# Residual sums and step-size sums as identity passes on TensorE, in a two-layer Metaformer kernel

## The chip, the cores and the metric

The kernel runs on one core of one Trainium2 chip. The metric is device time in microseconds; it is the time of one launch. The core has five engines that each work through their own queue in order: TensorE (PE), VectorE (DVE), ScalarE (ACT), GpSimd (POOL) and SyncE (SP), which issues the transfers.

## The reference

The input is an image batch `x` of shape (4, 64, 64, 128), float32. Two layers follow, each of a mixing part and a feed-forward part, all with residuals:

```python
x = x + L0_conv(ln_c(x))      # state-space scans over the image in 4 directions
t = tokens(x)
t = t + L0_ffn(ln_t(t))       # 64 experts with a global gate: top 8 tokens pooled and scattered
x = image(t)
x = x + L1_conv(ln_c(x))      # self, row-sum and column-sum projections
t = tokens(x)
t = t + L1_ffn(ln_t(t))       # 16 spectral filters of length 4096, and 3 shifted projections
```

In the scans each of 4 directions has 256 channels with 16 states and 4096 positions. The step size of a channel at a position is a softplus, and the state follows a recurrence:

```python
delta = softplus(dts + dt_bias)
h = exp(delta * A) * h + (delta * u) * B     # for each of 16 states
y = sum over states of h * C
```

## The kernel before, in words

**Stages.** Each image passes through `before_scans` (norm, projection, 3x3 convolution, projections to B, C and the step sizes' inputs), `gate`, the scans, `after_scans` (sum of directions, norm, gate, projection to 128 channels, residual), `experts_and_sums` (gate, pooled tokens, experts, scatter with a residual, then layer 1's mixing with a residual and the shifted projections), `to_slots`, the filters (`convolve`) and `from_slots`. Only `before_scans(0)` runs alone at the head. Then come the scans of all four images, and beside image b's scans runs a list of other stages, `beside(b)` (L1262): beside image 0 the first stages of images 1 to 3, `gate` for images 0 to 2 and `filters()`, which only prepares constants; beside image b > 0 the stages `after_scans`, `experts_and_sums` and `to_slots` of image b - 1, and then eight groups of `convolve`. "The filters" below means `convolve`. After the scans, in the tail, image 3's later stages run among the other 40 groups of `convolve`.

**The scans.** They are cut into 128 chunks (4 images x 4 directions x 8 pieces of 512 positions), each with 16 steps, one for each state; the loop over the 2048 steps starts at L1395. In a step s: SP loads `bc` for s + 5; ACT makes `da` for s + 3 (L1412, two halves, five buffers); DVE multiplies `db` = `du` x B (L1440) and runs two recurrences into `hh` (L1446, six buffers); POOL saves the last state of step s - 1 (L1455) and multiplies its `hh` by C (L1456); PE adds step s - 2 into `y` in PSUM by transposing passes (L1482). At the end of a chunk ACT copies `dx` of the next chunk into `du` in PSUM (`into_psum`, L1389); `du` and `db` have one buffer each.

**The step sizes.** `step_sizes` (L1292) makes the next chunk's `dl` (step sizes) and `dx` (`dl` times the channel's input `xc`) in small pieces, one at the start of each step from step 1 on: transfers at step 1; two projections on PE (L1311) with two reads by ACT each (L1315, L1316) at steps 2 and 3; three ACT operations of width 1024 at steps 4 to 6; at step 7 a POOL subtraction `ex` (L1337) and ACT's Ln into `w` (L1338); at step 8 POOL's `w` + `ex` (L1340); at step 9 POOL's `dl` + `w` (L1342); at step 10 POOL's product `dx` (L1344). The next chunk's first `da` is issued at step 13.

**Dealing.** The stages are generators that yield a weight after each piece of work. `deal` (L1361) is called twice a step, in the middle and at the end of the step's passes into `y`; it hands out pieces until an image's share is due, and orders them behind the step's own instructions on each engine. The share is `WEIGHT[b]` (L35), the sum of a list's weights, spread over the deals. The first chunk of an image and steps 2 and 3 of every chunk (`FIRST`, `BUSY`) get none; there `deal` returns at its top, before anything else.

**PSUM beside the scans.** `slots(ones, twos)` (L209) gives the dealt stages two single banks (`ones`), or one double bank (`twos`) in `convolve`, which switches at its beginning and its end. `bank` (L232) hands out a bank. An eviction from PSUM is put in a list by `evict_soon` (L226) and queued later by `settle` (L222), at the next deal or the next bank.

**Residuals.** Three residuals are POOL additions of an evicted projection: in `after_scans` `project` (L563) evicts to `pr` and L590 adds it to `xr`, which is then stored to `x1_d`; in `experts_and_sums` `scatter` (L929) evicts to `sc` and L950 adds it to `x2`; `mix` (L979) evicts to `zs` and L1041 adds it to `x2`. `pipelined` (L278) runs each such list of steps as a software pipeline over the row groups, the later steps first.

Of the kernel before, what the change touches and what calls it, by code (L numbers as in the profile page):

```python
# [17 lines left out]
P = 128  # L18
# [10 lines left out]
SC = 512  # L29
# [2 lines left out]


FIRST = 1
WEIGHT = (1346.0, 2087.0, 2005.0, 2059.0)  # L35

BUSY = (2, 3)

# [40 lines left out]
def kernel(  # L79
# [126 lines left out]

    side = {"tail": False, "deals": False}

    def slots(ones, twos):  # L209
        if "pool" in side:  # L210
            side["pool"].close()
        side["pool"] = ExitStack()
        for name, n in (("ones", ones), ("twos", twos)):
            side[name] = n and side["pool"].enter_context(
                tc.tile_pool(name=f"side_{name}", bufs=n, space=PSUM)
            )

    soon = []  # L220
# [5 lines left out]
    def evict_soon(work):  # L226
        if side["deals"]:
            soon.append(work)
        else:
            work()  # L230

    def bank(shape, name):  # L232

# [273 lines left out]
    def after_scans(b):  # L507

        with tc.tile_pool(name="po", bufs=2) as po:
            yk, y, z, xr, st, yT, pr = {}, {}, {}, {}, {}, {}, {}  # L510

            def rows(g):
                return slice(256 * g, 256 * (g + 1))

            def load(g):
                for k in range(K):
                    t = po.tile([P, 2, DI], F32, name=f"yk{k}")
                    yk[g, k] = t
                    if k % 2 == 0:
                        src = y_d[b][k, rows(g), :].rearrange("(q p) d -> p q d", p=P)  # L520
                        nc.sync.dma_start(t, src)
                    else:
                        byc = y_d[b][k].rearrange("(w q i) d -> i w q d", w=W, i=2)
                        for i in range(2):
                            nc.sync.dma_start(
                                t[i * W : (i + 1) * W], byc[i][:, 2 * g : 2 * g + 2]
                            )

            def add(g):
                ps = bank([P, 2, DI], "yk_ps")  # L530
                for k in range(K):
                    nc.tensor.matmul(ps, ident, yk.pop((g, k)), start=(k == 0), stop=(k == K - 1))  # L532
                y[g] = po.tile([P, 2, DI], F32, name="y", bufs=8)
                evict_soon(lambda: evict(y[g], ps))

            def sums(g):
                st[g] = norm_sums(po, y[g], 2, DI, eps5)

            def apply(g):
                z[g] = po.tile([P, 2, 256], F32, name="z", bufs=5)  # L540
                nc.sync.dma_start(z[g], z_d[b][:, :, rows(g)].rearrange("h p l -> p h l"))
                xr[g] = po.tile([P, 2, C], F32, name="xr", bufs=9)
                nc.sync.dma_start(xr[g], x[b, rows(g), :].rearrange("(q p) c -> p q c", p=P))
                norm_apply(y[g], y[g], st[g], 2)

            def turn(g):
                yT[g] = po.tile([P, 2, 256], F32, name="yT", bufs=4)
                ps = bank([P, 2, 2, P], "yt_ps")
                for h in range(2):
                    for q in range(2):  # L550
                        nc.tensor.transpose(
                            ps[:, h, q, :], y[g][:, q, h * P : (h + 1) * P], ident
                        )
                for h in range(2):
                    nc.scalar.activation(
                        yT[g][:, h, :],
                        ps[:, h].rearrange("p q t -> p (q t)"),
                        AF.Identity,
                        bias=nb[:, h : h + 1],
                        scale=nw[:, h : h + 1],  # L560
                    )

            def project(g):  # L563
                ps = bank([P, 2, C], "pr_ps")
                for q in range(2):
                    for h in range(2):
                        nc.tensor.matmul(
                            ps[:, q, :],
                            yT[g][:, h, q * P : (q + 1) * P],
                            w_out_t[:, h, :],  # L570
                            start=(h == 0),
                            stop=(h == 1),
                        )
                pr[g] = po.tile([P, 2, C], F32, name="pr")
                evict_soon(lambda: evict(pr[g], ps))

            yield from pipelined(
                16,
                (1.0, load),
                (2.2, add),  # L580
                (2.0, sums),
                (1.2, lambda g: norm_refine(po, st[g], 2, DI, 1e-5)),
                None,
                (1.2, apply),
                None,
                (1.0, turn),
                (1.2, lambda g: nc.gpsimd.tensor_mul(yT[g], yT[g], z[g])),
                None,
                (1.2, project),
                (0.7, lambda g: nc.gpsimd.tensor_add(xr[g], xr[g], pr[g])),  # L590
                (
                    0.4,
                    lambda g: nc.sync.dma_start(
                        x1_d[b][rows(g), :].rearrange("(q p) c -> p q c", p=P), xr[g]
                    ),
                ),
            )
# [114 lines left out]
    def experts_and_sums(b):  # L712

        with tc.tile_pool(name="mk", bufs=1) as kp:
# [203 lines left out]
            with tc.tile_pool(name="l1", bufs=2) as lp:  # L918
# [2 lines left out]
                mm = lp.tile([P, H], F32, name="mm", bufs=1)  # L921
                mk = lp.tile([P, 2, W], F32, name="mk", bufs=1)
                with tc.tile_pool(name="l1a", bufs=2) as la:
                    sc, st, xn = {}, {}, {}

                    def x4(g):
                        return x2[:, 4 * g : 4 * g + 4, :]

                    def scatter(g):  # L929
                        ps = bank([P, 4, C], "sc_ps")  # L930
                        for q in range(4):
                            t0 = 512 * g + q * P
                            nc.tensor.matmul(
                                ps[:, q, :], pT[:, t0 : t0 + P], outE, start=True, stop=True
                            )
                        sc[g] = la.tile([P, 4, C], F32, name="sc")
                        evict_soon(lambda: evict(sc[g], ps))

                    def sums(g):
                        st[g] = norm_sums(la, x4(g), 4, C, eps6)  # L940
# [1 line left out]
                    def apply(g):  # L942
# [3 lines left out]
                    yield from pipelined(  # L946
                        8,
                        (0.4, lambda g: nc.sync.dma_start(x4(g), tiles(x1_d[b], g))),
                        (1.5, scatter),
                        (1.2, lambda g: nc.gpsimd.tensor_add(x4(g), x4(g), sc[g])),  # L950
                        (3.0, sums),
                        (1.2, lambda g: norm_refine(la, st[g], 4, C, 1e-6)),
                        None,
# [17 lines left out]
                yield LAG  # L971

                with tc.tile_pool(name="l1b", bufs=2) as lb:
                    zs, st2, u, uT, ar = {}, {}, {}, {}, {}

                    def x2g(g):
                        return x2[:, 2 * g : 2 * g + 2, :]

                    def mix(g):  # L979
                        ps = bank([P, 2, C], "z_ps")  # L980
                        for q in range(2):
                            r0 = 4 * g + 2 * q
                            pq = ps[:, q, :]
                            t0 = r0 * W
                            nc.tensor.matmul(pq, xT[:, t0 : t0 + P], wself_t, start=True, stop=False)  # L985
                            nc.tensor.matmul(
                                pq, mk.rearrange("p i w -> p (i w)"), wk_t, start=False, stop=False
                            )
                            for i in range(2):
                                nc.tensor.matmul(  # L990
                                    pq[i * W : (i + 1) * W],
                                    mm[:, r0 + i : r0 + i + 1].to_broadcast([P, W]),
                                    wm_t,
                                    start=False,
                                    stop=True,
                                )
                        zs[g] = lb.tile([P, 2, C], F32, name="zs")
                        evict_soon(lambda: evict(zs[g], ps))

                    def sums2(g):  # L1000
                        st2[g] = norm_sums(lb, x2g(g), 2, C, eps5)
# [15 lines left out]
                    def regress(g):  # L1017
# [19 lines left out]

                    yield from pipelined(
                        16,
                        (1.8, mix),  # L1040
                        (0.7, lambda g: nc.gpsimd.tensor_add(x2g(g), x2g(g), zs[g])),  # L1041
                        (1.6, sums2),
                        (1.2, lambda g: norm_refine(lb, st2[g], 2, C, 1e-5)),
                        None,
# [235 lines left out]
    with ExitStack() as c0:  # L1280
# [11 lines left out]
        def step_sizes(b, k, ci):  # L1292
# [6 lines left out]
            def pieces():  # L1299
# [37 lines left out]
                nc.gpsimd.tensor_sub(ex, ex, dx)  # L1337
                nc.scalar.activation(w, w, AF.Ln)  # L1338
                yield
                nc.gpsimd.tensor_add(w, w, ex)  # L1340
                yield
                nc.gpsimd.tensor_add(dl, dl, w)  # L1342
                yield
                nc.gpsimd.tensor_mul(dx, dl, xc)  # L1344

            return dl, dx, xc, pieces()
# [14 lines left out]
        def deal(*behind):  # L1361


            if i % (K * NSC) < FIRST or s >= total or s % N in BUSY:
                return
            start = len(traced)
            settle()
            share["due"] += WEIGHT[chunks[i][0]] / ((K * NSC - FIRST) * (N - len(BUSY)) * 2)
            while share["made"] < share["due"]:
                share["made"] += next(share["pieces"], 1e9)  # L1370
# [256 lines left out]
```

## Time and profile before

| | |
|---|---|
| Runs | 11200.63, 11200.73, 11202.45 us; median 11200.73 |
| Profiled execution | 11189.8 us |
| Its span, first to last instruction | 11188.0 us |
| Mean granted TensorE clock | 0.83 |
| Busy: PE | 8372.3 us (75%) |
| Busy: DVE | 8145.9 us (73%) |
| Busy: ACT | 6173.9 us (55%) |
| Busy: POOL | 7262.3 us (65%) |
| Scan steps, first to last | about 290 to 9006 us |
| `convolve` beside the scans | about 3600 to 4640, 5700 to 6800, 7860 to 9006 us |

An engine's busy time is the time in which it works on an instruction. In the views, a line such as `hh L1446` names the tile that is written and the line of the kernel; `A <- B` means that A waited until B was done; in a list of waits the numbers are the total in us, how many there were, and the longest. In a timeline each row has the start, the duration, the engine, the line, what is written from what, the shape and how many instructions were merged; square brackets hold the idle time just before it and what ended it. A row of 40 digits is the busy share, in tenths, in 40 equal slices of the span.

### The profile page before, as it was taken

What the parts mean: (1) busy time and instruction counts of PE and PEld (TensorE: products, weight loads), DVE (VectorE), ACT (ScalarE), POOL (GpSimd) and SP (SyncE); (2) the same over time, 40 slices, a digit from 0 to 9 for tenths busy, and PEclk for the clock granted to TensorE, in tenths of its full rate; (3) what the DMA queues carried; (4) which work ended last, traced back from release to release, by engine and by line L of the source; (5) the groups of instructions that cost most, each with busy time, mean ns of one, the idle gap of its engine ahead of it and who ended that gap; (6) DMA issues with size and microseconds to landing.
All of it is one profiled execution on the core that took longest, in us unless ns stands there. A gap on an engine that the chain in (4) does not pass through costs nothing. (4 is left out here: it accounts for less than half of the span.)

```text
span 11188.0 us, 117102 instructions
## 1 busy us (share of the span) xinstructions
PE 8372.3 (75%) x34656; PEld 4820.6 (43%) x34656; DVE 8145.9 (73%) x7046; ACT 6173.9 (55%) x12043; POOL 7262.3 (65%) x6518
## 2 busy tenths in 40 slices
PE   6677676546766777657677776576677789999999
PEld 2444443334454444444543344455344444355443
DVE  0898988887887999879878898798699933222222
ACT  4667566657566665674655566647456534124222
POOL 1878787888787878788877788778687821001001
PEclk9787777757776888778778887687788899999999
DMA  2465656657556666657565566574666664553555
GB/s 98 161 206 178 200 174 209 191 179 217 203 200 185 187 193 193 201 174 240 172 185 168 170 194 205 159 262 155 188 193 193 189 155 125 150 136 94 143 131 123
DMA packets 901458, 1980.14 MB, mean 177 GB/s; under 512 B 101563, under 2 KB 415579, under 8 KB 899291
## 3 DMA queue, kind: packets, MB, share of 16 engines
q1 hardware_dynamic: 900826, 1972.65, 58.3%
q8 instruction: 283, 4.64, 0.2%
q14 instruction: 349, 2.85, 0.1%
HBM read 1766.77 MB, written 205.52 MB: 176 GB/s over the span
## 5 line engine op out<-in xcount | busy, mean ns | idle before, releaser
L1456 POOL TENSOR_TENSOR hh<-hh,bc 128x1024 f32<-128x1024 f32 x2048 | 4829.5, 2359 | 417.4 <-DVE hh L1446 190.5
L1446 DVE TENSOR_TENSOR_SCAN hh<-da,hst,db 128x512 f32<-128x512 f32 x3584 | 4392.2, 1266 | 528.8 <-PE y L1482 146.6
L1412 ACT ACTIVATE da<-dl,aneg 128x512 f32<-128x512 f32 x4096 | 2765.3, 717 | 2006.7 <-DVE hh L1446 1922.1
L1482 PE MATMUL y<-ident,hh 128*128 128x128 f32 x16384 | 2783.7, 320 | 1092.7 <-POOL hh L1456 980.7
L1482 PEld LDWEIGHTS y<-ident,hh 128*128 128x128 f32 x16384 | 2288.6, 166 | 2452.9 <-POOL hh L1456 1290.6
L1440 DVE TENSOR_TENSOR db<-du,bc 128x1024 f32<-128x1024 f32 x2048 | 2523.2, 1232 | 733.8 <-ACT du L1393 627.3
L1142 PE MATMUL cv_ps<-slab,us 64*128 64x512 f32 x4096 | 1164.0, 674 | 528.0 <-ACT y L256 298.5
L256 ACT COPY y<-cv_ps 128x512 f32<-128x512 f32 (+1 forms) x1024 | 755.3, 742 | 687.3 <-PE cv_ps L1142 658.6
L1163 PE MATMUL zq_ps<-y,me 128*128 128x512 f32 x2048 | 1006.1, 612 | 42.5 <-ACT y L256 37.5
L1455 POOL COPY hst<-hh 128x2 f32<-128x2 f32 x1792 | 338.8, 189 | 1052.4 <-DVE hh L1446 948.1
L1163 PE MATMUL zq_ps<-y,mo 128*128 128x512 f32 x2048 | 973.1, 599 | 0.0
L254 DVE COPY y<-cv_ps 128x512 f32<-128x512 f32 x640 | 441.3, 691 | 559.5 <-PE cv_ps L1142 509.4
L1142 PEld LDWEIGHTS cv_ps<-slab,us 64*128 64x128 f32 x4096 | 398.9, 201 | 981.8 <-ACT y L256 387.2
L1179 POOL TENSOR_TENSOR zt<-zt,zt 128x512 f32<-128x512 f32 x64 | 81.2, 1269 | 1007.3 <-DVE zt L254 531.4
L1446 DVE TENSOR_TENSOR_SCAN hh<-da,db 128x512 f32<-128x512 f32 x512 | 596.9, 1208 | 64.4 <-PE y L1482 29.7
L410 PE MATMUL cv_ps<-xh,diag 128*128 128x512 f32 x1152 | 534.3, 607 | 0.9 <-ACT sg_v L352 0.8
L1163 PEld LDWEIGHTS zq_ps<-y,me 128*128 128x128 f32 x2048 | 353.4, 194 | 379.1 <-issue 266.1
L1163 PEld LDWEIGHTS zq_ps<-y,mo 128*128 128x128 f32 x2048 | 358.3, 192 | 316.2 <-issue 313.3
L1311 PE MATMUL dt_ps<-dts,dtw 8*128 8x512 f32 x512 | 352.8, 804 | 180.7 <-ACT sg_v L352 54.6
L254 DVE COPY zt<-zq_ps 128x512 f32<-128x512 f32 x39 | 26.9, 691 | 529.8 <-PE zq_ps L1163 524.2
L1337 POOL TENSOR_TENSOR ex<-ex,dx 128x1024 f32<-128x1024 f32 x128 | 302.9, 2366 | 147.1 <-ACT dx L1334 146.8
L532 PE MATMUL yk_ps<-yk,ident 128*128 128x512 f32 x512 | 278.4, 689 | 92.1 <-ACT y L256 37.6
(222 smaller groups left out, 8714.4 us busy)
## 6 DMA issues: line engine op xcount, KB each, us to landing
bc<-bc_d SPq DMA_DIRECT2D x2048, 512.0 KB
slab<-hd SPq DMA_DIRECT2D x1024, 256.0 KB
xc<-xc_d SPq DMA_DIRECT2D x128, 512.0 KB
y_d<-ys SPq DMA_DIRECT2D x128, 512.0 KB
w1t<-in_w_dram SPq DMA_DIRECT2D x128, 512.0 KB
w2t<-in_w_dram SPq DMA_DIRECT2D x256, 256.0 KB
xc_x<-xc_d SPq DMA_DIRECT2D x64, 512.0 KB
yk<-y_d SPq DMA_DIRECT2D x128, 256.0 KB
```

The costliest lines, as they stand in the source:

```text
L254: nc.vector.tensor_copy(dst, src)
L256: nc.scalar.copy(dst, src)
L410: nc.tensor.matmul(ps, diag[:, h, t, :], xh[:, 8 * g + dy : 8 * g + dy + 8, dx : dx + W], start=(t == 0), stop=(t == 8),)
L1142: nc.tensor.matmul(pq[q].rearrange("p (r k t) -> p r k t", r=2, t=BS), us[b, G][rows, p, a if e == 0 else 1 - a, :], slab[i][rows, p, :, : ...
L1163: nc.tensor.matmul(z, (me, mo)[e][:, KQ * kq + k, :], ys[e][:, :, :, :, k, :].rearrange("p a q r t -> p (a q r) t"), start=(e == 0 and k = ...
L1311: nc.tensor.matmul(ps, dtw[:, k, h * P : (h + 1) * P], dts, start=True, stop=True)
L1412: i_act = nc.scalar.activation(das[t][:, h, :], sizes[t // N][0][:, h, :], AF.Exp, scale=aneg[:, tk, h, t % N : t % N + 1],)
L1440: nc.vector.tensor_mul(db, dus[i], bcs[s][:, 0:1, :].to_broadcast([P, 2, SC]))
L1446: i_dve = nc.vector.tensor_tensor_scan(o, d0, d1, init, ALU.mult, ALU.add)
L1455: nc.gpsimd.tensor_copy(hsts[t // N][:, :, t % N], hhs[t][:, :, last])
L1456: i_pool = nc.gpsimd.tensor_mul(hhs[t], hhs[t], bcs.pop(t)[:, 1:2, :].to_broadcast([P, 2, SC]))
L1482: i_pe = nc.tensor.matmul(ys[c][:, q, h, :], hhs[t][:, h, q * P : (q + 1) * P], ident, is_transpose=True, start=(n == 0 and k > 0 and q % ...
```

## The change

Three things are done, and three follow from them.

The residuals no longer take a POOL addition. `project`, `scatter` and `mix` first pass the residual's rows through the identity into the PSUM bank, one pass for the whole bank, and the projections accumulate on top; the eviction then writes the sum, in `scatter` and `mix` straight into `x2`. The steps with the POOL additions go from the pipelines, and `x1_d` is stored from `pr`.

The step sizes' sum `dl` + `ex` + `w`, where `side["ones"]` holds (that is, not beside `convolve`), is made by three identity passes of 512 columns for each half, into a bank of its own, at steps 8 and 9; ACT copies each bank to `dl`. Beside `convolve` both POOL additions stay.

`deal` now settles before it can return, so also in an image's first chunk and in steps 2 and 3. `slots` settles before it gives its banks back. Buffers change (`xr` 9 to 7, `pr` 2 to 4; `sc` and `zs` are gone), and so do the weights of the changed steps, with `WEIGHT`.

```diff
-WEIGHT = (1346.0, 2087.0, 2005.0, 2059.0)
+WEIGHT = (1346.0, 2070.0, 1989.0, 2042.0)
...
     def slots(ones, twos):
         if "pool" in side:
+            settle()
             side["pool"].close()
...
-                xr[g] = po.tile([P, 2, C], F32, name="xr", bufs=9)
+                xr[g] = po.tile([P, 2, C], F32, name="xr", bufs=7)
...
             def project(g):
                 ps = bank([P, 2, C], "pr_ps")
+                nc.tensor.matmul(ps, ident, xr[g], start=True, stop=False, skip_group_check=True)
                 for q in range(2):
                     for h in range(2):
                         nc.tensor.matmul(
                             ps[:, q, :],
                             yT[g][:, h, q * P : (q + 1) * P],
                             w_out_t[:, h, :],
-                            start=(h == 0),
-                            stop=(h == 1),
+                            start=False,
+                            stop=(q == 1 and h == 1),
+                            skip_group_check=True,
                         )
-                pr[g] = po.tile([P, 2, C], F32, name="pr")
+                pr[g] = po.tile([P, 2, C], F32, name="pr", bufs=4)
                 evict_soon(lambda: evict(pr[g], ps))
...
-                (1.2, project),
-                (0.7, lambda g: nc.gpsimd.tensor_add(xr[g], xr[g], pr[g])),
+                (1.4, project),
                 (
                     0.4,
                     lambda g: nc.sync.dma_start(
-                        x1_d[b][rows(g), :].rearrange("(q p) c -> p q c", p=P), xr[g]
+                        x1_d[b][rows(g), :].rearrange("(q p) c -> p q c", p=P), pr[g]
...
                     def scatter(g):
                         ps = bank([P, 4, C], "sc_ps")
+                        nc.tensor.matmul(
+                            ps, ident, x4(g), start=True, stop=False, skip_group_check=True
+                        )
...
-                        sc[g] = la.tile([P, 4, C], F32, name="sc")
-                        evict_soon(lambda: evict(sc[g], ps))
+                        evict_soon(lambda: evict(x4(g), ps))
...
-                        (1.5, scatter),
-                        (1.2, lambda g: nc.gpsimd.tensor_add(x4(g), x4(g), sc[g])),
+                        None,
+                        (2.2, scatter),
...
                     def mix(g):
                         ps = bank([P, 2, C], "z_ps")
+                        nc.tensor.matmul(
+                            ps, ident, x2g(g), start=True, stop=False, skip_group_check=True
+                        )
...
-                        zs[g] = lb.tile([P, 2, C], F32, name="zs")
-                        evict_soon(lambda: evict(zs[g], ps))
+                        evict_soon(lambda: evict(x2g(g), ps))
...
-                        (1.8, mix),
-                        (0.7, lambda g: nc.gpsimd.tensor_add(x2g(g), x2g(g), zs[g])),
+                        (2.2, mix),
...
-                nc.gpsimd.tensor_add(w, w, ex)
-                yield
-                nc.gpsimd.tensor_add(dl, dl, w)
-                yield
+                if side["ones"]:
+
+                    for h in range(2):
+                        ps = bank([P, SC], "dl_ps")
+                        for t in (dl, ex, w):
+                            nc.tensor.matmul(ps, ident, t[:, h], start=t is dl, stop=t is w)
+                        evict_soon(lambda h=h, ps=ps: nc.scalar.copy(dl[:, h], ps))
+                        yield
+                else:
+                    nc.gpsimd.tensor_add(w, w, ex)
+                    yield
+                    nc.gpsimd.tensor_add(dl, dl, w)
+                    yield
                 nc.gpsimd.tensor_mul(dx, dl, xc)
...
         def deal(*behind):
+            start = len(traced)
+            settle()
             if i % (K * NSC) < FIRST or s >= total or s % N in BUSY:
                 return
-            start = len(traced)
-            settle()
```

More of the change, by code (lines that the diff above doesn't have):

```diff
@@ L207 @@
     side = {"tail": False, "deals": False}
[L209 to L216, printed above, removed]
     soon = []
@@ L230, in evict_soon, with slots @@
             work()
+    def slots(ones, twos):
+        if "pool" in side:
+            settle()
+            side["pool"].close()
+        side["pool"] = ExitStack()
+        for name, n in (("ones", ones), ("twos", twos)):
+            side[name] = n and side["pool"].enter_context(
+                tc.tile_pool(name=f"side_{name}", bufs=n, space=PSUM)
+            )
     def bank(shape, name):
@@ L923, in experts_and_sums @@
                 with tc.tile_pool(name="l1a", bufs=2) as la:
-                    sc, st, xn = {}, {}, {}
+                    st, xn = {}, {}
                     def x4(g):
@@ L933, in scatter @@
                             nc.tensor.matmul(
-                                ps[:, q, :], pT[:, t0 : t0 + P], outE, start=True, stop=True
-                            )
-                        sc[g] = la.tile([P, 4, C], F32, name="sc")
-                        evict_soon(lambda: evict(sc[g], ps))
+                                ps[:, q, :],
+                                pT[:, t0 : t0 + P],
+                                outE,
+                                start=False,
+                                stop=(q == 3),
+                                skip_group_check=True,
+                            )
+                        evict_soon(lambda: evict(x4(g), ps))
                     def sums(g):
@@ L973, in experts_and_sums @@
                 with tc.tile_pool(name="l1b", bufs=2) as lb:
-                    zs, st2, u, uT, ar = {}, {}, {}, {}, {}
+                    st2, u, uT, ar = {}, {}, {}, {}
                     def x2g(g):
@@ L980, in mix @@
                         ps = bank([P, 2, C], "z_ps")
+                        nc.tensor.matmul(
+                            ps, ident, x2g(g), start=True, stop=False, skip_group_check=True
+                        )
                         for q in range(2):
@@ L984, in mix @@
                             t0 = r0 * W
-                            nc.tensor.matmul(pq, xT[:, t0 : t0 + P], wself_t, start=True, stop=False)
                             nc.tensor.matmul(
-                                pq, mk.rearrange("p i w -> p (i w)"), wk_t, start=False, stop=False
+                                pq,
+                                xT[:, t0 : t0 + P],
+                                wself_t,
+                                start=False,
+                                stop=False,
+                                skip_group_check=True,
+                            )
+                            nc.tensor.matmul(
+                                pq,
+                                mk.rearrange("p i w -> p (i w)"),
+                                wk_t,
+                                start=False,
+                                stop=False,
+                                skip_group_check=True,
                             )
@@ L994, in mix @@
                                     start=False,
-                                    stop=True,
-                                )
-                        zs[g] = lb.tile([P, 2, C], F32, name="zs")
-                        evict_soon(lambda: evict(zs[g], ps))
+                                    stop=(q == 1),
+                                    skip_group_check=True,
+                                )
+                        evict_soon(lambda: evict(x2g(g), ps))
                     def sums2(g):
```

## The prediction

> **What bounds the kernel now.** I read the page first, then the busy time by stage, then VectorE's waits, and last the order of instructions around one of these waits. The page's rows for VectorE, ScalarE, GpSimd and the granted clock, over 40 slices of 280 us:
>
> ```profile
> DVE  0898988887887999879878898798699933222222
> POOL 1878787888787878788877788778687821001001
> PEclk9787777757776888778778887687788899999999
> ```
>
> DVE and POOL are high until slice 32, then PE alone is full: two regimes. The busy time by stage (us busy, instructions in brackets, then clock, DMA share, GB/s) for image 0's scans, the first half of images 1, 2 and 3, one second half, and the tail:
>
> ```profile
> 290.00:2480.00 2190.00, 1435.26 (x5784) 903.76 (x5784) 1927.63 (x1592) 1409.77 (x2608) 1800.97 (x1414) 0.75 0.58 188
> 2480.00:3600.00 1120.00, 768.84 (x3878) 534.90 (x3878) 927.41 (x761) 712.82 (x1647) 901.04 (x928) 0.76 0.62 200
> 3600.00:4640.00 1040.00, 766.28 (x3262) 432.06 (x3262) 975.40 (x799) 631.55 (x909) 836.82 (x577) 0.85 0.62 189
> 4640.00:5700.00 1060.00, 727.62 (x3730) 516.96 (x3731) 889.48 (x732) 666.38 (x1564) 858.50 (x905) 0.76 0.62 198
> 6800.00:7860.00 1060.00, 726.33 (x3751) 516.33 (x3750) 904.27 (x744) 672.06 (x1568) 868.10 (x906) 0.76 0.61 198
> 9006.00:11188.00 2182.00, 2113.46 (x7109) 941.80 (x7108) 542.38 (x782) 688.77 (x1625) 260.66 (x532) 0.98 0.53 133
> ```
>
> The third column of busy times is DVE, the fifth POOL. An undisturbed scan step takes 3.85 us of DVE (one db at 1.23, two scans at 1.27, gaps), so 2048 steps need 7885 us; the scans run from 290 to 9006, 8716 us. About 80 us of the difference are DVE's side reductions, the rest, some 750, are stalls. The second half of image 1 (filters beside the scans) is nearly free of them (975 busy of 1040). In the four other stages DVE is idle 262, 193, 171 and 156 us, while POOL is at 80 to 82%. What DVE waited for, in the first halves of images 2 and 3:
>
> ```profile
> DVE db L1440 <- ACT du L1393: 76.5, 9, 16.8
> DVE db L1440 <- ACT du L1393: 53.4, 7, 15.4
> ```
>
> du is copied by ACT at the end of a chunk; ACT itself is 65% busy. The timeline of one such wait, at a chunk's end in image 0:
>
> ```profile
> 2195.79 2.45 DVE L1446 TENSOR_TENSOR_SCAN hh<-da,hst,db 128x512 f32<-128x512 f32 x2
> 2204.62 1.23 DVE L1440 TENSOR_TENSOR db<-du,bc 128x1024 f32<-128x1024 f32 x1 [6.38 <-ACT du L1393]
> ...
> 2176.22 2.36 POOL L1340 TENSOR_TENSOR w<-w,ex 128x1024 f32<-128x1024 f32 x1
> 2178.52 0.19 POOL L1455 COPY hst<-hh 128x2 f32<-128x2 f32 x1
> 2178.66 2.35 POOL L1342 TENSOR_TENSOR dl<-dl,w 128x1024 f32<-128x1024 f32 x1
> 2180.98 2.34 POOL L1456 TENSOR_TENSOR hh<-hh,bc 128x1024 f32<-128x1024 f32 x1
> 2183.28 2.35 POOL L1344 TENSOR_TENSOR dx<-dl,xc 128x1024 f32<-128x1024 f32 x1
> ```
>
> POOL runs without a gap from there through the wait: late by its step-size work, it gives ACT and PE their inputs late, ACT reaches du late, DVE stands 6.38 us. I went through all DVE waits over 0.3 us and took POOL's busy share during each. In the four stages they sum to 576 us; with POOL over 90% busy during the wait, 260 us (92, 56, 54, 58). So under half is POOL's; the rest is ACT, PE or DMA in turns, with POOL idle too.
>
> **What the Trainium skill says.** "GPSIMD Engine Reference", section 3.1, puts a two-input elementwise operation at about 2.6 cycles an element; at its 1.2 GHz an estimate of 2.22 us for 1024 elements, and the trace has 2.36 (L1340, L1342), so nothing but removal helps. Its section 1 says GpSimd has no PSUM access, so each sum made on PE needs a copy by another engine; the trace agrees: every read of PSUM is by ACT or DVE. It also warns of a port shared with VectorE; here DVE's operations read one operand from PSUM, and the scans' spread is only 1245 to 1283 ns, so I credit no faster DVE. "TensorE: Matmul & The Clock Gate", Part 1, gives half clock to an array that was idle for a few us; the trace agrees, clock 0.75 in these stages, 0.98 in the tail.
>
> **The change part by part.**
> (1) *Step sizes.* In chunks outside the filters (image 0's 32 and about half of the 96 others, some 79 in all) two POOL adds go: 2.36 + 2.36 = 4.72 us a chunk, 373 us in all. Added: six identity passes of 128x512 and two ACT copies. The nearest row is the identity sum yk_ps (L532), 0.56 us busy each within the scans (215.1/384); 6 x 0.56 = 3.4 us of PE a chunk. The copies, at L256's 0.58, are 1.2 us of ACT. PE (65 to 70% busy) and ACT (64 to 67%) have room and neither is DVE's usual releaser, so I cost the busy time at nothing: what covers it is their idle time; uncovered, it would be 79 x 4.6 = 363 us. What counts is POOL's backlog. A du wait with POOL saturated shrinks by at most 4.7. Capping each of these waits at 4.7: image 0 has 17 of them, 62 us, capped 53.0; images 1 to 3 have 14, capped 20.7 + 26.6 + 14.1 = 61.4. Sum **114 us**. Where a wait is gone, DVE's 3.85 us step is next.
> (2) *Residuals within the scans.* POOL loses per image 16 x 0.73 (L590), 8 x 1.27 (L950), 16 x 0.73 (L1041) = 33.5 us, 100 in three images; they fall in the first halves, at about 2.7 us a chunk. They count only where the cap of 4.7 left something: nine waits over 7.4 us, 9 x 2.7 = **24 us**. Added: a pass of 0.56 or 0.28 us each, 13 us of PE an image, in PE's idle time. The eviction stays, with another target. The store to x1_d on SP now waits for ACT's eviction instead of POOL's add; bc loads are queued behind it, and DVE's waits for bc are only 35 us in all, so an earlier release is worth at most a few us: nothing. Fewer xr buffers, seven for nine, go with one stage less: nothing.
> (3) *New waits.* dx (POOL) now waits for ACT's second copy, which waits for PE, which waits for ex (POOL) and Ln (ACT). Behind dx on POOL stand hst and hh; PE's y passes wait for hh, DVE for their buffers. Between ex and dx POOL still has three hh (3 x 2.55 = 7.6 us), and PE plus ACT need 2 x (3 x 0.56 + 0.58) = 4.5 us. Bounds: 0 if all is hidden, 4.5 us if nothing is. I take 0.7 for each of the 31 saturated waits, **22 us lost**. Behind ACT's two copies stand da; da is issued three steps ahead, so a stop under 7.7 us costs DVE nothing.
> (4) *Settling in every deal.* Copies that were put off in a chunk's steps 2 and 3, and in the first chunk, are queued at once; the same instructions, at a place where ACT was waiting for DVE anyway (1910 us of such waits in all): nothing, within 10 us either way.
> (5) *WEIGHT* falls by 17 of about 2050, as the stages' own shares do, so the filters begin about 0.14 chunk earlier. In image 2 nine chunks of filters (5750 to 6320) each stall 6 to 12 us on du, in image 1 none do; it depends on how the filters' cycle meets the chunk. A shift can add or end three such stalls: plus or minus 25 us, central 0.
> (6) *Head.* For chunk 0 POOL's 4.7 us become about 3.2 on PE and ACT: **1.5 us gained**.
> (7) *Tail.* PE is 97% busy there and carries the chain of waits, so image 3's residual passes add in full: (8 + 32/2) x 0.49 (63.3/128 of L532 in the tail) = **12 us lost**; the freed POOL time is worth nothing there.
> Sum: 114 + 24 - 22 + 1.5 - 12 = 106 us gained. The profiled execution is 11189.8 (span 11188.0); it gives 11084. The median of the three runs is 10.9 longer, 11200.7; there it is **11095 us**. About 0.2%, 22 us, is what can be told from no change.
>
> **Rivals.**
> *POOL saturated but innocent*: in its place ACT's or PE's own lateness ends the waits. For it: 316 of 576 us of waits pass with POOL not full. Against it: waits like that at 2204, with POOL gapless. Time: only head and tail, 11200.7 + 10.5 = 11211.
> *A new wait takes half*: dx waits 2.2 us for the copies in each of the 31 chunks, 68 us instead of 22: 11141. For it: PE's queue there holds side passes at half clock.
> *ACT held too long, slower*: ACT's copies stand behind PE, PE behind POOL's ex, and da behind the copies. It decides once such a stop passes the lead of 7.7 us. If it costs DVE 2 us in each of 79 chunks, 158 us against 117 gained: 11200.7 + 41 + 10.5 = 11252. Against it: ex stands ahead of the hh that PE needs in any case.
> *More gain*: all saturated waits to the caps, half of the other 70 us, no new wait, filters well met: 114 + 24 + 35 + 25 - 12 = 186, 11015.
>
> **How the numbers follow.** Forecast (11060 to 11130) 0.50; more gain (below) 0.15; half (11130 to 11178) 0.20; innocent (within 22 us of now) 0.08; slower 0.07. So faster 0.85, same 0.08, slower 0.07. The range, 11015 to 11190, leaves out about 0.05 below and 0.13 above.
>
> **What would show it.** POOL busy falls by about 373 + 180 to 6710 us, PE rises by some 320, ACT by 92. The du waits of the four stages fall from 252 us to near 120; image 0's stage shortens by about 45 us; the span after the scans grows by 12. Wrong if du waits stay with POOL less full (innocent), if POOL shows idle time before dx (half), or if DVE's waits for da, now 80 us, pass 200 (slower).

## The result, and the profile after

The changed kernel takes 11041.34 us (median of four runs, 11036.41 to 11042.68) against 11200.68 before: a ratio of 0.9858, 95% interval 0.9845 to 0.9870. That is 159 us less; 106 were forecast. The time lies outside the forecast's own band (11060 to 11130) and inside its outer range (11015 to 11190), in the part that was called "more gain". The profiled execution fell from 11189.8 to 11042.2, by 147.6, and all comparisons of stages below are made between profiled executions.

The page's rows by slice, of the changed kernel:

```profile
DVE  0888989987897999989988899798799922222222
POOL 1777777877777878777777777677788711001001
PEclk9788888768887888878878888798888899999999
```

POOL has lost its eights where the other stages run beside the scans, and the granted clock of TensorE has gone up there. The stages follow, cut at the starts of the same chunks in both kernels: image 0's 32 chunks, then the first 16 chunks of images 1, 2 and 3 (columns as before). The prediction's windows do not end at chunks, and image 3's is too short: the filters beside it start at about 8005 us, not at 7860 as the table ahead of the prediction has it. First the kernel before:

```profile
297.00:2432.00 2135.00, 1407.75 (x5652) 882.91 (x5652) 1890.88 (x1561) 1379.47 (x2562) 1762.60 (x1388) 0.75 0.58 188
2432.00:3609.00 1177.00, 799.22 (x4028) 557.86 (x4028) 964.33 (x793) 745.04 (x1699) 942.73 (x955) 0.76 0.62 199
4602.00:5758.00 1156.00, 789.17 (x3972) 555.07 (x3971) 963.74 (x792) 718.56 (x1642) 925.22 (x940) 0.76 0.62 198
6815.00:7988.00 1173.00, 802.63 (x3969) 552.81 (x3969) 964.73 (x793) 723.03 (x1651) 933.52 (x962) 0.74 0.62 198
```

Then the changed kernel (its first row begins 7 us earlier, at the end of the head):

```profile
290.00:2402.00 2112.00, 1556.06 (x6030) 937.12 (x6029) 1887.66 (x1560) 1425.28 (x2638) 1622.59 (x1324) 0.79 0.58 191
2402.00:3544.00 1142.00, 858.07 (x4302) 569.33 (x4300) 965.26 (x794) 763.53 (x1735) 839.66 (x884) 0.83 0.65 206
4541.00:5665.00 1124.00, 855.59 (x4246) 569.35 (x4247) 964.47 (x793) 736.51 (x1675) 825.72 (x871) 0.82 0.65 203
6718.00:7856.00 1138.00, 854.15 (x4256) 558.90 (x4254) 964.50 (x792) 739.84 (x1684) 835.53 (x896) 0.82 0.64 204
```

Between the starts of the same chunks, image 0's stage fell from 2135 to 2105 us, the three first halves from 3506 to 3404 together, and the three halves beside the filters, which keep their additions, from 3069.5 to 3055.2. POOL's busy share in the three first-half rows is 73 to 74%, where it was 80%. The waits for du that were shown of images 2 and 3, now:

```profile
DVE db L1473 <- ACT du L1426: 31.7, 8, 12.9
DVE db L1473 <- ACT du L1426: 26.3, 6, 8.1
```

They were 76.5 and 53.4. Over the four stages (without the first wait, which is the head's) DVE's waits over 0.3 us were 641 us before and are 518 now. Those with POOL over 90% busy fell from 253 to 118, and all others rose a little, from 388 to 400.

But the new chain of waits is there too. The timeline of the changed kernel beside image 0's scans, in `gate`: TensorE's pass over `dl`, GpSimd's subtraction, TensorE's pass over its result, its last pass of that half, and ScalarE's copy:

```profile
2144.57 1.02 PE L1369 MATMUL dl_ps<-dl,ident 128*128 128x512 f32 x2
...
2151.07 2.35 POOL L1361 TENSOR_TENSOR ex<-ex,dx 128x1024 f32<-128x1024 f32 x1
...
2153.48 2.07 PE L1369 MATMUL dl_ps<-ex,ident 128*128 128x512 f32 x2 [4.64 <-POOL ex L1361]
...
2157.90 1.88 PE L1369 MATMUL dl_ps<-w,ident 128*128 128x512 f32 x2
2159.81 0.58 ACT L1370 COPY dl<-dl_ps 128x512 f32<-128x512 f32 x1 [7.81 <-PE dl_ps L1369]
```

PE stood 4.64 us for GpSimd's ex, and ACT stood 7.81 us for PE, with its later work behind it. The totals of the chain beside the scans (us, times, longest):

```profile
PEld dl_ps L1369 <- POOL ex L1361: 103.9, 37, 10.9
PE dl_ps L1369 <- POOL ex L1361: 80.9, 32, 10.6
...
POOL dx L1377 <- ACT dl L1370: 42.8, 18, 11.7
```

### The profile page after: what moved, and what is told of

Read it like the earlier page. It is cut to its first block, busy times and chain, and to the rows that moved or that the text cites. A ratio compares the mean times of both kernels' runs of the same rounds, so it can differ in the third digit from the quotient of the medians.

```text
span 11040.4 us, 119413 instructions
## 1 busy us (share of the span) xinstructions
PE 8697.3 (79%) x35936; PEld 4908.8 (44%) x35936; DVE 8146.2 (74%) x7046; ACT 6261.4 (57%) x12203; POOL 6771.4 (61%) x6198
## 5 line engine op out<-in xcount | busy, mean ns | idle before, releaser
L1515 PE MATMUL y<-ident,hh 128*128 128x128 f32 x16384 | 2655.8, 311 | 644.9 <-POOL hh L1489 538.5
L1515 PEld LDWEIGHTS y<-ident,hh 128*128 128x128 f32 x16384 | 2204.1, 161 | 2025.0 <-issue 1076.1
L317 POOL TENSOR_SCALAR no_a<-no_v 128x2 f32<-128x2 f32 (+1 forms) x224 | 43.0, 192 | 528.1 <-ACT no_sq L306 516.0
```

The source lines that it names most:

```text
L1515: i_pe = nc.tensor.matmul(ys[c][:, q, h, :], hhs[t][:, h, q * P : (q + 1) * P], ident, is_transpose=True, start=(n == 0 and k > 0 and q % ...
```

## Which part carries the gain

The theory was that GpSimd's backlog makes DVE stand at the chunk's end, and that the step sizes are the larger part of it. The rivals were that the residuals carry it, that the early settling or the shifted filters do, and that TensorE's fuller clock does. Four kernels took the parts one by one.

**The step sizes alone.** The changed kernel with the residuals of before, and the dealing weights that go with them:

```diff
-                nc.tensor.matmul(ps, ident, xr[g], start=True, stop=False, skip_group_check=True)
...
+                (0.7, lambda g: nc.gpsimd.tensor_add(xr[g], xr[g], pr[g])),
...
+                        (1.2, lambda g: nc.gpsimd.tensor_add(x4(g), x4(g), sc[g])),
...
+                        (0.7, lambda g: nc.gpsimd.tensor_add(x2g(g), x2g(g), zs[g])),
```

> The changed kernel with the three residual additions, their pipelines and the weights as before: only the step sizes' sums go by TensorE, and the deals settle early. Theory (GpSimd's backlog sets the stalls, and the step sizes are the larger lump in it): about 11090 us, 110 below the kernel before (11200.7). Rival, residuals: if they carry the gain, 11170 or more. Rival, settling early or the shifted filters carry it: near 11041 too or at 11200, together with the kernel that only settles early.

Measured: 11069.5 us, ratio 0.9885 (0.9869 to 0.9902), beside 11196.4 for the kernel before on this chip: 127 us less. Image 0's stage is 2105 us, exactly that of the changed kernel; the first halves give 81 of their 102.

**The residuals alone.** The changed kernel with the additions of before in `step_sizes`:

```diff
-                if side["ones"]:
-                    for h in range(2):
...
+                nc.gpsimd.tensor_add(w, w, ex)
+                yield
+                nc.gpsimd.tensor_add(dl, dl, w)
+                yield
```

> The changed kernel with GpSimd's two step-size additions in every chunk: only the residuals, the weights and the early settling differ from before. Theory: about 11160 us, as GpSimd loses 100 us beside the scans but only part of it where it is late, and the tail pays some 10 to 20. Rival, residuals carry the gain: 11080 or less.

Measured: 11143.1, ratio 0.9952 (0.9937 to 0.9967), 53 us less. Image 0 stays at 2135, the first halves lose 42, the filters' halves 8. The two parts together would be 180; both at once give 159. That both take from the same backlog is a reading of this, not a separate measurement.

**Settling early, alone.** The kernel before with the new `deal` and `slots`:

```diff
+            start = len(traced)
+            settle()
             if i % (K * NSC) < FIRST or s >= total or s % N in BUSY:
                 return
-            start = len(traced)
-            settle()
```

> The kernel before with the early settling in the deals (first chunk, steps 2 and 3, and when banks are given back), nothing else. Theory: no work moves, 11190 to 11210 us. Rival, that evictions held back in steps 2 and 3 were what made ScalarE late at the chunk's end: 11100 or less.

Measured: 11194.7, ratio 0.9998 (0.9990 to 1.0007). Nothing comes from it.

**The pure relief.** The kernel before without the two additions outside the filters; it leaves out part of the softplus there:

```diff
-                nc.gpsimd.tensor_add(w, w, ex)
+                if not side["ones"]:
+                    nc.gpsimd.tensor_add(w, w, ex)
                 yield
-                nc.gpsimd.tensor_add(dl, dl, w)
+                if not side["ones"]:
+                    nc.gpsimd.tensor_add(dl, dl, w)
                 yield
```

> The kernel before, with GpSimd's two step-size additions left out beside all stages but the filters, so that the step size there is only the ReLU part, and nothing put in their place. It is the pure relief of GpSimd. Theory: 11060 to 11090 us, at or a little below the kernel with the step sizes by TensorE alone, the difference being what the passes and copies cost. Rival, a warmer TensorE clock carries the gain: TensorE has no more work here, so little gain, 11170 or more, and the clock stays at 0.83.

Measured: 11012.7, ratio 0.9833 (0.9818 to 0.9847), 184 us less, more than expected. The clock stayed at 0.836. So taking the work off GpSimd is worth up to 184 us, and TensorE's way of doing it gives 57 of them back. It is an upper bound, because this kernel also drops two links on the way to `dl` and `dx`.

## Is it GpSimd's load, or a warmer TensorE

**Passes that nobody reads.** The kernel before, all additions kept:

```diff
+                if side["ones"]:
+                    ps = bank([P, SC], "dl_ps")
+                    for t in range(3):
+                        nc.tensor.matmul(ps, ident, xc[:, 0], start=t == 0, stop=t == 2)
                 nc.gpsimd.tensor_add(w, w, ex)
```

(and the same over `xc[:, 1]` ahead of the second addition.)

> The kernel before with all of its GpSimd additions, and in the chunks outside the filters six identity passes of 512 columns at steps 8 and 9, over the chunk's input, whose sums nobody reads. Rival, a warmer TensorE clock (0.83 before, 0.864 changed) carries the gain: 11100 us or less. Theory, GpSimd's backlog: no gain, 11200 to 11240, the excess being what six passes cost when they wait for nothing late.

Measured: 11210.8 beside 11190.5, ratio 1.0015 (1.0008 to 1.0023). The clock rose to 0.854, most of the way to 0.864, and the kernel got slower by 17 to 20 us. The Trainium skill ("TensorE: Matmul & The Clock Gate", Part 1) has the clock follow TensorE's activity, and the trace agrees; but whatever the fuller clock buys here is less than what the passes that bring it cost.

**The load put back.** The changed kernel, and GpSimd makes two additions again, into a tile that is overwritten:

```diff
                         evict_soon(lambda h=h, ps=ps: nc.scalar.copy(dl[:, h], ps))
+                        nc.gpsimd.tensor_add(dx, xc, xc)
```

> The changed kernel with two GpSimd additions of the same size put back at steps 8 and 9 of the chunks outside the filters (into dx, which the product overwrites): TensorE's and ScalarE's new work stays, GpSimd's load is as before except for the residuals. Theory: the step sizes' gain is gone and the new waits stay, 11150 to 11200 us. Rival, something else than GpSimd's load carries it: 11080 or less.

Measured: 11135.3, ratio 0.9949 (0.9935 to 0.9964). That is the ratio of the residuals alone (0.9952): the step sizes' whole gain goes when GpSimd's load comes back, with every pass, copy and clock of the changed kernel in place. So the step sizes' gain is GpSimd's load, and neither the clock nor the early settling. The load was not quite put back: both inputs of these additions are `xc`, and they take 1.89 us each where those taken out took 2.36, so 303 us came back of the 377 that had gone. A longer time was expected, for the new waits. With a fifth of the load missing, how much those waits cost can't be read here.

## The tail

> The changed kernel with image 3's residuals, in the tail alone, added by GpSimd again. By the prediction's step (the tail pays its passes in full) 12 to 21 us less: 11020 to 11030. Rival, the tail hides them in TensorE's gaps and a fuller clock, as its length did not grow: within 6 us of the changed kernel, 11035 to 11047.

The edit puts image 3's residual additions back on GpSimd, in the tail alone. They stand in the step that follows the eviction, the store in `after_scans` and the norm's sums after `scatter` and `mix`, not in steps of their own:

```diff
-                nc.tensor.matmul(ps, ident, xr[g], start=True, stop=False, skip_group_check=True)
+                if not side["tail"]:
+                    nc.tensor.matmul(
+                        ps, ident, xr[g], start=True, stop=False, skip_group_check=True
+                    )
...
+            def store(g):
+                if side["tail"]:
+                    nc.gpsimd.tensor_add(pr[g], pr[g], xr[g])
```

Measured: 11026.9 beside 11190.5, ratio 0.9854 (0.9837 to 0.9870). By the medians of two chips that can't be told from the changed kernel (0.9858), so the profile has to say it. The last recurrence before, in the changed kernel, and in this one (duration in ns, shortest, median and longest, then first and last start):

```profile
L1446 DVE TENSOR_TENSOR_SCAN hh<-da,hst,db x3584: 1245/1267/1283, 357.6 to 9005.9; 128x512 f32<-128x512 f32 x200
```

```profile
L1479 DVE TENSOR_TENSOR_SCAN hh<-da,hst,db x3584: 1244/1269/1291, 357.8 to 8860.6; 128x512 f32<-128x512 f32 x200
```

```profile
L1498 DVE TENSOR_TENSOR_SCAN hh<-da,hst,db x3584: 1243/1268/1283, 359.0 to 8859.8; 128x512 f32<-128x512 f32 x200
```

From the end of the last recurrence to the end of the span (11188.0, 11040.4 and 11028.3) it is 2180.8, 2178.5 and 2167.2 us: the passes cost the tail 11.3. (The same pair with the subtraction on TensorE too, below, gives 14.6; kernels with an unchanged tail differ by up to 4.) So something else in the change took 13.6 us off the tail. The additions' own pipeline steps are gone in this kernel too, and the weights by which filters are dealt to the stages are smaller; which of the two it is was not tried.

## What TensorE's way costs, and a better one

**Passes without copies.** The kernel with the additions left out, plus six unread passes over `xc`; it leaves out the same part of the softplus:

```diff
+                for h, (o, t) in enumerate(((w, ex), (dl, w))):
+                    if side["ones"]:
+                        ps = bank([P, SC], "dl_ps")
+                        for j in range(3):
+                            nc.tensor.matmul(ps, ident, xc[:, h], start=j == 0, stop=j == 2)
```

> The kernel before with GpSimd's two additions left out outside the filters (so the step size there is only the ReLU part), and in their place six passes over the chunk's input whose sums nobody reads: TensorE's time without ScalarE's copies and without the chain of waits. It stands between two measured kernels: 0.9833 (additions left out, nothing in their place) and 0.9885 (sums by TensorE). If the cost is the chain of waits: 0.983 to 0.985. If it is TensorE's own time: 0.987 to 0.989.

Measured: 0.9855 (0.9842 to 0.9869), just above the range that the chain of waits was given. Against 0.9833 and 0.9885: of the 0.52% that TensorE's way costs, 0.22% (25 us) goes with the passes alone, 0.30% (34 us) with the copies and the chain of waits. The intervals are 0.13% wide to each side and two chips are compared, so the split is rough. The profiled executions agree: the four stages take 5482 us together with nothing in place of the additions, 5498 with the passes, 5530 with the sums by TensorE.

**A step later.** The changed kernel, one more step between the subtraction and the passes:

```diff
                 if side["ones"]:
-
+                    yield
                     for h in range(2):
                         ps = bank([P, SC], "dl_ps")
```

> The changed kernel with the six passes and the product dx a step later (passes at steps 9 and 10, dx at 11), outside the filters. Theory, that what the passes cost (0.5% between the kernel with the additions left out and the one with the sums by TensorE) is the new chain of waits: TensorE waits for GpSimd's ex, ScalarE for TensorE, GpSimd for ScalarE; a step more of room takes a good part away: 15 to 35 us under the changed kernel. Rival, the cost is the engines' time itself (5.2 us of passes, 1.2 us of copies a chunk) or a fixed due time at the chunk's end: within 8 us of it, or above.

> The changed kernel once more, as the reference for the three others on this chip. Both theories: 0.984 to 0.987 of the kernel before, as measured first (0.9858).

Measured, on one chip: 11044.0 for the changed kernel again (0.9863, 0.9849 to 0.9876), and 10993.4 with the step more (0.9819, 0.9805 to 0.9832): **51 us less**, more than expected, and the fastest kernel of the study. The chain of this kernel, in the same window:

```profile
PEld dl_ps L1369 <- POOL ex L1361: 44.2, 23, 10.8
PE dl_ps L1369 <- POOL ex L1361: 30.2, 19, 9.6
...
POOL dx L1377 <- ACT dl L1370: 26.6, 13, 7.4
```

TensorE's wait for ex is less than half, and GpSimd's for the copy fell from 42.8 to 26.6; ScalarE's for TensorE fell little, from 176.6 to 158.2. In the profiled execution image 0 takes 2090 (2105 changed) and the first halves 3379 (3404). What DVE gained is not at du, where its waits stay (111 and 107 us): its waits for TensorE's passes into y fell from 167 to 133. That fits a TensorE that no longer stands for ex ahead of those passes. But 51 us is more than the 34 that the split above leaves for copies and chain. The passes' own cost depends, it seems, on the step where they stand, and the split is not a sum of fixed prices.

**The subtraction by TensorE too.** One pass more for each half, through minus identity, and no GpSimd subtraction outside the filters:

```diff
-                nc.gpsimd.tensor_sub(ex, ex, dx)
+                if not side["ones"]:
+                    nc.gpsimd.tensor_sub(ex, ex, dx)
...
-                        for t in (dl, ex, w):
-                            nc.tensor.matmul(ps, ident, t[:, h], start=t is dl, stop=t is w)
+                        for t in (ex, dx, dl, w):
+                            m = minus if t is dx else ident
+                            nc.tensor.matmul(ps, m, t[:, h], start=t is ex, stop=t is w)
```

> The changed kernel with the subtraction ex - dx by TensorE as well, as a pass through minus identity: outside the filters four passes for each half instead of three, no GpSimd subtraction, and no wait of TensorE for GpSimd's ex. Theory: GpSimd loses another 80 x 2.36 = 189 us and the new wait is gone, 10980 to 11010 us. Rival, TensorE becomes the late engine in these stages (8 x 0.86 = 6.9 us a chunk): 11050 or more.

Measured: 11022.5 beside 11190.5, ratio 0.9851 (0.9836 to 0.9865): by the medians not told from the changed kernel; in the profile the scans take 8543 us against 8565. The expected 30 to 60 us did not come, though GpSimd lost another 178 us of busy time: image 0 stays at 2103, and GpSimd now waits 68.8 us for the copies (42.8 in the changed kernel). DVE's waits for du fell from 111 to 98, but those for TensorE's y rose from 167 to 185: part of the relief went into the two passes more. How much more GpSimd's time alone would be worth here was not measured.

**The subtraction by TensorE and the tail's residuals on GpSimd**, both edits as above, in one kernel:

> The changed kernel with the subtraction by TensorE too, outside the filters, and with image 3's residuals in the tail on GpSimd. If both edits save what they seemed to (some 10 us for the subtraction, some 5 to 14 for the tail), 15 to 25 us under the changed kernel on this chip. Rival, neither is real: within 8 us of it.

Measured: 11007.2, ratio 0.9832 (0.9819 to 0.9846), 37 us under the changed kernel on the same chip; tail 2164.0, scans 8546. Both savings add up, and more than was expected. The step more was not tried together with them.

## Why the prediction was right, and where a size was off

**The mechanism and its place** were right: waits under a saturated GpSimd fell by 135 us, the four stages by 131, and the load put back takes the step sizes' gain away. The du waits of the four stages were to fall from 252 to near 120 and fell to 111. "Settling in every deal" at nothing was right (0.9998). ScalarE's rise was to be 92 and is 88. GpSimd's busy time was to be 6710 and is 6771; the 180 us that the prediction took off for the residuals are not what its own prices give, 4 x 33.5 = 134.

**The sizes.** The scans lost 145.5 us, and steps (1) to (3) had put 116. Nearly all of the miss is in the step sizes. The relief measured 167 (8710 to 8543 with the additions left out), where step (1) had 114. What TensorE's way costs measured 47 (8543 to 8590), where step (3) had 22. Net that is 120 for 92.

**Step (1), 114 us**, is where the sum was most wrong: it capped du waits alone and put every other wait at nothing. With the additions left out, image 0 loses 63 and the first halves 96, 159 in all (the filters' halves another 8). Of DVE's waits there, those for du fell by only 84 us, less than the cap. All its others fell by 75: for da by 14, for transfers by 14, for GpSimd's own results by 17, and for ScalarE's results in the other stages by 27; those for y stayed (2). Nor was all of it saturated time: of the 158 us, 109 were waits with GpSimd over 90% busy.

**Step (3)** was costed as a wait of GpSimd at dx, and that is only 42.8 us in all; the longer waits are earlier in the chain, TensorE for ex and ScalarE for TensorE (176.6 us, 58 times). A price was misread too. One pass of 128x512 shows as two rows of the trace, so six passes are 12 rows. At 0.86 us a pass where the clock is full, that is 5.2 us a chunk; at the clock granted, 6.8 were measured (541 us in 80 chunks), twice the 3.4 of the prediction. The Trainium skill would have shown it: "FP8 and Floating Point Precision", TensorE Precision Notes, counts four passes through the array for true FP32, and 4 x 512 columns at the 2.4 GHz of "TensorE: Matmul & The Clock Gate" make an estimate of 0.85 us, as measured.

**Step (2), 24 us**, counted what the residuals add once the step sizes' waits are capped, and that is 26 (8590 against 8565). Alone they give 49.

**By place**: in image 0 the change gave less than forecast (30 for 45), in the first halves more (102). **Step (5)**, the filters' shift at 0, plus or minus 25: their halves lost 14 us. That it is the shift isn't shown, as the step sizes alone, with the weights of before, lost 9 there.

**Step (7), 12 us lost** in the tail, measured 11 to 15, but by luck: the same price of one row for a pass is in it. With both rows, 8 x 0.86 + 32 x 0.43 = 21 us would have been lost "in full", and the tail did not pay that. And what took 13.6 us off the tail had no place in the sum, so the span after the scans did not grow. **TensorE's rise**, to be some 320 and measured 325, is luck too: the new rows take 660 us, and TensorE's other work shrank by about as much as the misread price had left out. **Step (6)**, the head, was to gain 1.5; the first db starts at 297.2 instead of 297.0, and over the runs of the study this start moves by several us: nothing to be seen.

So the sum missed by 41 us in the profiled execution: 29 in the scans, 14 in the tail, less 2 in the head.

**The rivals.** "Innocent" fell with the load put back. "Slower" fell: da waits are 67 us, not 200. "Half" was partly there, as the chain above, but the relief was larger too. "More gain" (11015) came nearest beside the forecast, though not as it was put: the relief went beyond the caps, but the new waits were not nothing.

## What to carry to other kernels

An engine with slack on average (GpSimd at 80%) can still hold the loop where its work comes in lumps ahead of a deadline; look at its busy share during each stall, and price a lump by all the stalls that it may stand behind, not by one kind of them. Work that moves to another engine through PSUM becomes a chain of in-order waits over three engines: give it a step of room between producer and consumer, which here was worth 51 us, a third of the whole change. Putting the old load back beside the new code is a strong proof of where a gain comes from; measure the load that was put back, which here was a fifth short.

## What the runs showed that was not expected

A float32 pass of 128x512 leaves two rows in the trace, whose starts are 0.43 us apart at full clock, so 0.86 us a pass; one transposing pass of 128x128 leaves one. GpSimd's addition of 128x1024 took 1.89 us where both inputs were the same tile, and 2.36 where they were two. The clock granted to TensorE over the whole run went from 0.83 to 0.854 by 960 added rows of unread passes, and the run became 0.15% longer all the same. With 660 us of new rows (541 for the sums, the rest for the residuals) TensorE's busy time rose by only 325: its passes into y took 2656 us instead of 2784, and other groups shrank too, while the granted clock went from 0.83 to 0.864.
